# Attention row sums through adding DMAs, maxima subtracted in every step, and roots by a power operation

## The chip, the core and the metric

The kernel runs on one core of a Trainium2 chip. The metric is the device time of one execution in microseconds, as the median of several runs. Engines are named as in the profile: PE is the matrix engine (PEld its weight loads), DVE the vector engine, ACT the scalar engine, POOL the GpSimd engine, SP the engine that issues most DMAs.

## The reference

A decoder layer over x of shape 2 x 2048 x 512 (two batches), in three residual parts. All arithmetic is in f32.

```
h = layernorm(x)                         # mean and variance over 512, eps 1e-5, no weights
Q, K = rope(h Wq^T), rope(h Wk^T)        # 16 heads of 32
V = h Wv^T
x = x + softmax(Q K^T / sqrt(32)) V Wo^T # all 2048 keys, no mask
x = x + gelu_tanh(layernorm(x) ctx^T) ctx    # ctx: 77 x 512 per batch
x = x + clip((layernorm(x) sign(Wf)^T) * scale + bias, -100, 100)
```

## The kernel before

Each batch is worked in two phases. The first, `project_batch`, goes over 16 chunks of 128 rows: normalise, transpose, multiply with the three weights, rotate, and store queries and keys transposed (heads on partitions) in four blocks of 512 columns. The second, `Attention.run`, is the long one.

Attention is cut into 32 units per batch. A unit is a block of 256 queries and a group `g` of four heads. A unit has eight steps; a step treats two chunks of 128 keys for the four heads, in two half-steps (heads 0 and 1, then heads 2 and 3). In a half-step

- `lower` (L501) writes the negated row maxima of the unit into the tile `st` by a small bf16 matmul with ones, where the step asks for it,
- `scores` (L516) accumulates keys times queries on top of it, 128 keys by 256 queries per head and chunk,
- `maxima` (L423) computes scores the other way round (128 queries by 512 keys) for a step ten steps ahead, and DVE reduces them to row maxima (L435),
- ACT takes the exponential of `st` into `pw` (L643), a pool of three buffers,
- POOL adds the two chunks of `pw` into `sm` (L645),
- PE multiplies the weights `pw` of the step before with the values into `acc` (`weigh`, L534).

The row sums of the softmax are the columns of `acc` that `total` (L548) fills: it multiplies `sm` with ones. One half of the 256 columns is done in each half-step, two steps behind. For the last step of a unit the whole 256 columns are done at once. `divide` then copies `acc`, takes reciprocals on DVE (L568) and multiplies on POOL (L571).

To write the maxima only in steps 0 and 4 of a unit, the kernel goes through the keys in an order (`chunk`) in which step 1 takes a chunk of the next key block, and multiplies there with the difference of the two blocks' keys (`key_steps`, L474). Added to the scores already in `st`, that gives the new chunk's scores. The three difference tiles lie in the buffers of the weights wk, wq and wv, so these are loaded again for the second batch.

The maxima of the next unit are split in step 5. DVE reduces them, POOL splits them into three bf16 parts (L444 to L448), and a transposing DMA on SP's queue (L455) turns them into `mrow`, which `lower` reads from the start of the next unit.

The third part, `after_attention`, is everything behind the attention for a block of 512 rows: the output projection, the two norms, the two small networks. It is a generator in a queue; `background` runs one piece of it in each step, and in every other step a further light piece. Its elementwise work lies on POOL as long as attention runs (`side`).

The order on PE, DVE, ACT and POOL in the attention loop is the program order, written by hand (`manual_schedule`).

Roots of the variance are computed without ACT: `rstd_seed` makes a first guess by integer arithmetic on DVE, and `rstd_step` is a Newton step of four operations, taken three times, on POOL (in the last blocks of the program on DVE).

Of the kernel before, what the change touches and what calls it, by code (L numbers as in the profile page):

```python
# [10 lines left out]
BF16 = mybir.dt.bfloat16  # L11
U32 = mybir.dt.uint32
I32 = mybir.dt.int32
AF = mybir.ActivationFunctionType
# [3 lines left out]
P = 128  # L18
# [4 lines left out]
BLK = 512  # L23
# [4 lines left out]
NU = NB * ND * 2  # L28
STEPS = NCH // 2
AHEAD = STEPS + 2  # L30
SCALE = 1.0 / math.sqrt(DK)
# [6 lines left out]
def decoder_layer(  # L38
# [21 lines left out]
    big = ctx.enter_context(tc.tile_pool(name="big", bufs=3))  # L60
    sums = ctx.enter_context(tc.tile_pool(name="sums", bufs=3))
    work = ctx.enter_context(tc.tile_pool(name="work", bufs=5))
# [15 lines left out]


    def load_qkv():  # L80
        return [load_w(w, name) for w, name in ((wk_t, "wk"), (wq_t, "wq"), (wv_t, "wv"))]

    x_next = [load_x(0, 0), load_x(0, 1)]
    qkv = load_qkv()
    cos = const.tile([P, NCH, DK // 2], F32, tag="cos", name="cos")
# [10 lines left out]
    ones = const.tile([P, DK], F32, tag="ones", name="ones")  # L96
    nc.vector.memset(ones, 1.0)


# [32 lines left out]

    def rstd_seed(var, n):
        v = small.tile([P, n], F32, tag=f"v{n}", name="v")
        nc.vector.tensor_scalar(v, var, 1.0, EPS, ALU.mult, ALU.add)
        y = small.tile([P, n], F32, tag=f"rstd{n}", name="rstd")
        t = small.tile([P, n], F32, tag=f"t{n}", name="t")
        nc.vector.tensor_scalar(t.bitcast(I32), v.bitcast(I32), 1, None, ALU.arith_shift_right)
        nc.vector.tensor_scalar(
            y.bitcast(I32), t.bitcast(I32), -1.0, float(0x5F3759DF), ALU.mult, ALU.add  # L140
        )
        return v, y, t

    def rstd_step(engine, v, y, t):
        engine.tensor_mul(t, y, y)
        engine.tensor_mul(t, t, v)
        engine.tensor_scalar(t, t, -0.5, 1.5, ALU.mult, ALU.add)
        engine.tensor_mul(y, y, t)

    def project_batch(b, ahead, att, wk, wq, wv):

        def norm(ch):
            xc = ahead.pop(0)
            if ch + 2 < NCH:
                ahead.append(load_x(b, ch + 2))
            mv = small.tile([P, 2], F32, tag="mv1", name="mv")
            chunk_stats(xc, mv)  # L160
            v, y, t = rstd_seed(mv[:, 1:2], 1)
            for _ in range(3):
                rstd_step(nc.gpsimd, v, y, t)
            off = small.tile([P, 1], F32, tag="off1", name="off1")
            nc.gpsimd.tensor_mul(off, mv[:, 0:1], y)
            nc.gpsimd.tensor_scalar(off, off, -1.0, None, ALU.mult)
            xn = work.tile([P, D], F32, tag="w", name="xn")
            nc.scalar.activation(xn, xc, AF.Identity, bias=off, scale=y)
            return xn
# [93 lines left out]
        att.turn_maxima(0)  # L263
        att.key_steps()

# [18 lines left out]
    def after_attention(b, blk, ot, first, end):  # L284
# [19 lines left out]
        def norm(mv):  # L304
            v, y, t = rstd_seed(mv[:, :, 1], n)
            yield False
            for _ in range(3):
                rstd_step(side(), v, y, t)
                yield False
            off = small.tile([P, n], F32, tag=f"off{n}", name="off")  # L310
            side().tensor_mul(off, mv[:, :, 0], y)
            side().tensor_scalar(off, off, -1.0, None, ALU.mult)
            yield False
            yield False
            for c in range(n):
                xn = work.tile([P, D], F32, tag="w", name="xn2")
                nc.scalar.activation(
                    xn, xs[c], AF.Identity, bias=off[:, c : c + 1], scale=y[:, c : c + 1]
                )
                yield True  # L320
                pt = bank([P, ND, P], "pt2")
                for i in range(ND):
                    nc.tensor.transpose(pt[:, i, :], xn[:, i * P : (i + 1) * P], ident)  # L323
                nc.scalar.copy(ot[:, :, chunks[c]], pt)
                yield c + 1 == n
# [71 lines left out]
    class Attention:  # L397
# [67 lines left out]


        def key_steps(self):
            self.dk = [None] + [
                const.tile([P, ND, BLK], F32, tag=f"w{n}", name=f"dk{n}") for n in "kqv"
            ]  # L470

            def differences(g):
                for kb in range(1, NB):
                    nc.gpsimd.tensor_sub(  # L474
                        self.dk[kb][:, g, :], self.k[kb][:, g, :], self.k[kb - 1][:, g, :]
                    )
                    yield False

            def others():
                for g in range(1, ND):  # L480
                    for _ in differences(g):
                        for _ in range(4):
                            yield False

            for _ in differences(0):
                pass
            queue.append(others())


        @staticmethod  # L490
        def chunk(i, c):
            return (i % NB) * CPB + (i // NB) * 2 + c

        def lower(self, u, heads):
# [13 lines left out]
        def scores(self, u, i, heads, c):  # L510
            qb, g, hf = self.units[u]
            kb, kc = divmod(self.chunk(i, c), CPB)
            keys = self.dk[kb] if kb else self.k[kb]
            for h in heads:
                r = self.rows[h]
                nc.tensor.matmul(  # L516
                    self.st[h][:, c, :],
                    keys[r, g, kc * P : (kc + 1) * P],
                    self.q[qb][r, g, hf * HQ : (hf + 1) * HQ],
                    start=False,  # L520
                    stop=True,
                    skip_group_check=True,
                )


        def weigh(self, step, c):
            u, i, pw, sm = step
            qb, g, hf = self.units[u]
# [3 lines left out]
            for h in range(4):  # L532
                d0 = g * P + h * DK
                nc.tensor.matmul(  # L534
                    acc[self.rows[h], 0, :],
                    self.v[self.chunk(i, c)][:, d0 : d0 + DK],
                    pw[:, h, c, :],
                    start=(i == 0 and c == 0),
                    stop=(i == STEPS - 1 and c == 1),
                    skip_group_check=True,  # L540
                )


        def total(self, step, part):
            u, i, pw, sm = step
            acc = self.acc[u]
            for h in range(4):
                nc.tensor.matmul(  # L548
                    acc[self.rows[h], 1, part],
                    ones,  # L550
                    sm[:, h, part],
                    start=False,
                    stop=(i == STEPS - 1),
                    skip_group_check=True,
# [40 lines left out]
        def run(self):  # L595
            prev = None
            sums_due = None
            ends = []
# [5 lines left out]
            def first_half():  # L604
                if prev is not None:
                    self.weigh(prev, 0)
                if sums_due is not None:
                    self.total(sums_due, slice(0, P))

            def second_half():  # L610
                nonlocal sums_due
                if prev is not None:
                    self.weigh(prev, 1)
                if sums_due is not None:
                    self.total(sums_due, slice(P, HQ))
                sums_due = prev
                if prev is not None and prev[1] == STEPS - 1:
                    self.total(prev, slice(0, HQ))
                    ends.append(self.divide(prev[0]))
                    sums_due = None  # L620

# [10 lines left out]
            for t in range(NU * STEPS):  # L632
                u, i = divmod(t, STEPS)
                pw = big.tile([P, 4, 2, HQ], F32, tag="s", name="pw")
                sm = sums.tile([P, 4, HQ], F32, tag="sm", name="sm")
                for heads, others in (((0, 1), (2, 3)), ((2, 3), (0, 1))):
                    if i % NB == 0:
                        self.lower(u, heads)
                    self.scores(u, i, heads, 0)
# [6 lines left out]
                    if reduce:  # L646
                        reduce()
                    if heads[0] == 0:
                        first_half()
# [5 lines left out]
                    else:  # L655
# [7 lines left out]
                        background(1)  # L663
                prev = (u, i, pw, sm)
            first_half()
# [6 lines left out]
    for b in range(B):  # L672
        att = Attention(b)
        project_batch(b, x_next, att, *qkv)
        if b == 0:
# [3 lines left out]
        if b + 1 < B:  # L679
            x_next = [load_x(b + 1, 0), load_x(b + 1, 1)]  # L680
            qkv = load_qkv()
    alone.append(True)
# [50 lines left out]
```

## Time and profile before

| | us |
|---|---|
| median of 3 runs | 2804.71 (2804.29 to 2805.34) |
| the profiled execution | 2803.13 |
| its span, first to last instruction | 2801.0 |
| granted clock of PE, mean | 0.997 |
| loop of the second batch, by the timeline | 1616 to 2755 |

Busy time of an engine is the union of its instructions' spans. Matmul spans overlap in the pipeline, so the time that a matmul costs is read from the distance of starts, not from its own length. f32 matmuls appear as two records each. A row of the timeline gives start, length, engine, line and operation, the tiles, how many instructions are merged into it, and in brackets how long the engine was idle before it and who ended that.

### The profile page before, as it was taken

The numbers are of one execution on the slowest core, as the hardware profiler recorded it, in microseconds if no ns is written. First come the engines' busy times: TensorE is split into PE (matmuls) and PEld (weight loads), VectorE is DVE, ScalarE is ACT, GpSimd is POOL, SyncE is SP. The second block draws the span as 40 slices with busy tenths as digits, with TensorE's granted clock in tenths as the row PEclk, the third lists the DMA queues.
The fourth block names the chain that finished last, engine by engine and source line by source line (L and its number), as shares of the span: only waits on it lengthen the run. The fifth ranks groups of instructions, "written<-read, shape, count | busy, mean of one in ns | idle before, by whom it ended". The sixth has DMA issues, their size and how long they took to land.

```text
span 2801.0 us, 70846 instructions
## 1 busy us (share of the span) xinstructions
PE 2762.5 (99%) x30748; PEld 1490.8 (53%) x30748; DVE 1714.5 (61%) x3003; ACT 1319.9 (47%) x2391; POOL 1804.3 (64%) x2393
## 2 busy tenths in 40 slices
PE   8999999999999999999999999999999999999997
PEld 4445555555555555555444455555555555555553
DVE  4436777666666766665244467766766666666644
ACT  1114555455546544654322155555555455545542
POOL 4326767567757685767644287766777566857772
PEclk9999999999999999999999999999999999999998
DMA  4000000000100010000201000000000000000000
GB/s 136 20 19 2 5 4 4 4 4 7 30 3 4 4 33 4 4 4 33 72 24 31 15 4 4 4 4 4 4 17 20 4 4 11 26 4 4 18 11 16
DMA packets 41864, 43.56 MB, mean 16 GB/s; under 512 B 24759, under 2 KB 24759, under 8 KB 41553
## 3 DMA queue, kind: packets, MB, share of 16 engines
q1 hardware_dynamic: 41552, 39.05, 4.7%
q8 instruction: 240, 3.93, 0.6%
q14 instruction: 72, 0.58, 0.1%
HBM read 26.58 MB, written 8.39 MB: 12 GB/s over the span
## 4 chain that ended last, share of the span: by engine, by line
PE 96%; DVE 2%; POOL 1%; issue 1%; ACT 0%; DMA 0%; ACTq 0%; DVEq 0%; POOLq 0%
PE st L516 21%; PE acc L534 21%; PE ps L423 18%; PE acc L548 8%; PE pf L363 4%; PE pk L181 4%; PE po L329 4%; PE pv L181 4%; PE pq L181 4%; PE st L501 3%; PE pt L323 1%; PE po L355 1%; PE ph L336 1%; PE ptqk L189 1%; PE pt L174 1%
## 5 line engine op out<-in xcount | busy, mean ns | idle before, releaser
L645 POOL TENSOR_TENSOR sm<-pw 128x512 f32<-128x512 f32 x1024 | 1297.6, 1271 | 628.4 <-ACT pw L643 624.2
L435 DVE TENSOR_REDUCE mx<-ps 128x1 f32<-128x512 f32 x2048 | 1311.8, 682 | 566.6 <-PE ps L423 563.9
L643 ACT ACTIVATE pw<-st 128x512 f32<-128x512 f32 x2048 | 1111.3, 595 | 1004.0 <-PE ps L423 665.9
L423 PE MATMUL ps<-k,q 32*128 32x512 f32 x4096 | 1221.6, 639 | 2.2 <-ACT v L198 1.1
L534 PE MATMUL acc<-pw,v 128*32 128x256 f32 x8192 | 655.6, 391 | 0.0
L548 PE MATMUL acc<-sm,ones 128*32 128x128 f32 x7680 | 392.2, 280 | 1.4 <-POOL sm L645 1.4
L423 PEld LDWEIGHTS ps<-k,q 32*128 32x128 f32 x4096 | 359.4, 183 | 46.7 <-issue 24.3
L534 PEld LDWEIGHTS acc<-pw,v 128*32 128x32 f32 x8192 | 162.4, 108 | 402.3 <-issue 383.2
L548 PEld LDWEIGHTS acc<-sm,ones 128*32 128x32 f32 x7680 | 248.7, 110 | 157.2 <-POOL sm L645 2.7
L516 PE MATMUL st<-q,dkq 32*128 32x256 f32 x2048 | 291.4, 401 | 0.0
L516 PE MATMUL st<-q,dkk 32*128 32x256 f32 x2048 | 291.0, 400 | 0.0
L516 PE MATMUL st<-q,dkv 32*128 32x256 f32 x2048 | 289.9, 400 | 0.0
L516 PE MATMUL st<-q,k 32*128 32x256 f32 x2048 | 265.5, 375 | 0.0
L516 PEld LDWEIGHTS st<-q,dkk 32*128 32x128 f32 x2048 | 175.4, 184 | 90.1 <-issue 48.0
L516 PEld LDWEIGHTS st<-q,dkq 32*128 32x128 f32 x2048 | 172.2, 184 | 79.9 <-issue 55.2
L516 PEld LDWEIGHTS st<-q,dkv 32*128 32x128 f32 x2048 | 174.7, 184 | 68.8 <-issue 37.3
L516 PEld LDWEIGHTS st<-q,k 32*128 32x128 f32 x2048 | 194.4, 187 | 13.6
L214 POOL TENSOR_TENSOR r<-r 128x512 f32<-128x512 f32 x64 | 81.0, 1267 | 184.6 <-DVE r L213 167.0
L568 DVE RECIPROCAL num<-num 128x128 f32<-128x128 f32 x128 | 120.5, 943 | 64.2 <-ACT num L562 64.2
L190 ACT COPY q<-ptqk 128x512 f32<-128x512 f32 x32 | 18.9, 590 | 222.6 <-PE ptqk L189 222.6
L181 PE MATMUL pk<-wk,xnt 128*128 128x512 f32 x256 | 119.7, 611 | 2.7 <-ACT xnt L176 2.7
L363 PE MATMUL pf<-wf,q 128*128 128x512 f32 x256 | 119.1, 609 | 0.0
(99 smaller groups left out, 1963.9 us busy)
## 6 DMA issues: line engine op xcount, KB each, us to landing
x<-in_x_dram SPq DMA_DIRECT2D x64, 256.0 KB, 2.7
out_dram<-x SPq DMA_DIRECT2D x32, 256.0 KB, 2.0
wk<-in_wk_t_dram SPq DMA_DIRECT2D x2, 1024.0 KB, 5.3
wq<-in_wq_t_dram SPq DMA_DIRECT2D x2, 1024.0 KB, 8.0
wv<-in_wv_t_dram SPq DMA_DIRECT2D x2, 1024.0 KB, 12.9
wo<-in_wo_t_dram SPq DMA_DIRECT2D x1, 1024.0 KB, 7.0
wf<-in_wf_t_dram SPq DMA_DIRECT2D x1, 1024.0 KB, 9.1
mrow<-mt SPq DMA_TRANSPOSE x62, 2.3
```

Of the source, the lines that this page charges most:

```text
L181: nc.tensor.matmul(dst, xnt[:, i, :], w[:, i, :], start=(i == 0), stop=(i == ND - 1))
L329: nc.tensor.matmul(ps, ot[:, i, cols], wo[:, i, :], start=(i == 0), stop=(i == ND - 1))
L363: nc.tensor.matmul(pf, ot[:, i, cols], wf[:, i, :], start=(i == 0), stop=(i == ND - 1))
L423: nc.tensor.matmul(ps, self.q[qb][self.rows[h], g, q0 : q0 + P], self.k[kb][self.rows[h], g, :], start=True, stop=True,)
L435: nc.vector.tensor_reduce(mx[:, qc, h, kb : kb + 1], ps, AX.X, ALU.max)
L501: nc.tensor.matmul(self.st[h], ones_b[r, :], mrow[r, None, :].to_broadcast([DK, 2, HQ]), start=True, stop=False, skip_group_check=True,)
L516: nc.tensor.matmul(self.st[h][:, c, :], keys[r, g, kc * P : (kc + 1) * P], self.q[qb][r, g, hf * HQ : (hf + 1) * HQ], start=False, stop=Tr ...
L534: nc.tensor.matmul(acc[self.rows[h], 0, :], self.v[self.chunk(i, c)][:, d0 : d0 + DK], pw[:, h, c, :], start=(i == 0 and c == 0), stop=(i ...
L548: nc.tensor.matmul(acc[self.rows[h], 1, part], ones, sm[:, h, part], start=False, stop=(i == STEPS - 1), skip_group_check=True,)
L568: nc.vector.reciprocal(num[:, 1, part], num[:, 1, part])
L643: nc.scalar.activation(pw[:, h], self.st[h], AF.Exp, scale=SCALE)
L645: nc.gpsimd.tensor_add(sm[:, hs, :], pw[:, hs, 0, :], pw[:, hs, 1, :])
```

## The change

- `total` is no longer called two steps behind. In step 0 POOL's sums go into a tile `first` (one buffer). In steps 1 to 5 they go into `sm` (two buffers), and a DMA issued on POOL's queue adds `sm` into `first` in SBUF. Steps 6 and 7 keep their `sm`. When the unit ends, PE takes the total of `first` in the first half of the next unit's step 0, and those of steps 6 and 7 in the second half, each over all 256 columns.
- `lower` runs in every step. Keys are used as they are, in their own order. `key_steps` is gone, and the weights stay in their buffers for the second batch.
- A root is one addition of eps, one power operation with exponent -0.5 on POOL, and the two operations for the shift. `rstd_seed` and `rstd_step` are gone.

The diff, cut to its core:

```diff
+COLLECTED = STEPS - 2
...
-    sums = ctx.enter_context(tc.tile_pool(name="sums", bufs=3))
+    chain = ctx.enter_context(tc.tile_pool(name="chain", bufs=1))
+    summed = ctx.enter_context(tc.tile_pool(name="summed", bufs=2))
...
+    def scale_and_shift(engine, mv, n):
         y = small.tile([P, n], F32, tag=f"rstd{n}", name="rstd")
+        engine.tensor_scalar(y, mv[:, :, 1], EPS, None, ALU.add)
+        nc.gpsimd.tensor_tensor(y, y, minus_half[:, :n], ALU.pow)
+        off = small.tile([P, n], F32, tag=f"off{n}", name="off")
+        engine.tensor_mul(off, mv[:, :, 0], y)
+        engine.tensor_scalar(off, off, -1.0, None, ALU.mult)
+        return y, off
...
-            kb, kc = divmod(self.chunk(i, c), CPB)
-            keys = self.dk[kb] if kb else self.k[kb]
+            kb, kc = divmod(2 * i + c, CPB)
...
-        def total(self, step, part):
-            u, i, pw, sm = step
+        def total(self, u, sm, last=False):
             acc = self.acc[u]
             for h in range(4):
                 nc.tensor.matmul(
-                    acc[self.rows[h], 1, part],
+                    acc[self.rows[h], 1, :],
                     ones,
-                    sm[:, h, part],
+                    sm[:, h, :],
...
             def first_half():
                 if prev is not None:
                     self.weigh(prev, 0)
-                if sums_due is not None:
-                    self.total(sums_due, slice(0, P))
+                    if prev[1] == STEPS - 1:
+                        self.total(prev[0], due.pop(0))
 
             def second_half():
...
                 if prev is not None:
                     self.weigh(prev, 1)
-                if sums_due is not None:
-                    self.total(sums_due, slice(P, HQ))
...
+                    if prev[1] == STEPS - 1:
+                        while due:
+                            self.total(prev[0], due.pop(0), last=not due)
+                        ends.append(self.divide(prev[0]))
...
-                sm = sums.tile([P, 4, HQ], F32, tag="sm", name="sm")
+                if i == 0:
+                    first = sm = chain.tile([P, 4, HQ], F32, tag="ch", name="first")
+                else:
+                    sm = summed.tile([P, 4, HQ], F32, tag="sm", name="sm")
                 for heads, others in (((0, 1), (2, 3)), ((2, 3), (0, 1))):
-                    if i % NB == 0:
-                        self.lower(u, heads)
+                    self.lower(u, heads)
...
                     nc.gpsimd.tensor_add(sm[:, hs, :], pw[:, hs, 0, :], pw[:, hs, 1, :])
                     if reduce:
                         reduce()
+                    if heads[0] == 2 and 0 < i < COLLECTED:
+                        nc.gpsimd.dma_start(out=first, in_=sm, accum_op=ALU.add)
...
-                prev = (u, i, pw, sm)
+                prev = (u, i, pw)
+                if i == 0 or i >= COLLECTED:
+                    due.append(sm)
```

More of the change, by code (lines that the diff above doesn't have):

```diff
@@ L11 @@
 BF16 = mybir.dt.bfloat16
-U32 = mybir.dt.uint32
-I32 = mybir.dt.int32
 AF = mybir.ActivationFunctionType
@@ L77, in load_w @@
         return t
-    def load_qkv():
-        return [load_w(w, name) for w, name in ((wk_t, "wk"), (wq_t, "wq"), (wv_t, "wv"))]
     x_next = [load_x(0, 0), load_x(0, 1)]
-    qkv = load_qkv()
+    wk = load_w(wk_t, "wk")
+    wq = load_w(wq_t, "wq")
+    wv = load_w(wv_t, "wv")
     cos = const.tile([P, NCH, DK // 2], F32, tag="cos", name="cos")
@@ L97, in decoder_layer @@
     nc.vector.memset(ones, 1.0)
+    minus_half = const.tile([P, CPB], F32, tag="minus_half", name="minus_half")
+    nc.vector.memset(minus_half, -0.5)
     mts = []
@@ L130, in chunk_stats, with project_batch @@
         nc.vector.bn_aggr(mv, st)
-    def rstd_seed(var, n):
-        v = small.tile([P, n], F32, tag=f"v{n}", name="v")
-        nc.vector.tensor_scalar(v, var, 1.0, EPS, ALU.mult, ALU.add)
+    def scale_and_shift(engine, mv, n):
         y = small.tile([P, n], F32, tag=f"rstd{n}", name="rstd")
[L137 to L153, printed above, removed]
+        engine.tensor_scalar(y, mv[:, :, 1], EPS, None, ALU.add)
[4 more added lines that the diff above has]
+        return y, off
+    def project_batch(b, ahead, att):
         def norm(ch):
@@ L158, in norm @@
                 ahead.append(load_x(b, ch + 2))
[L159 to L166, printed above, removed]
+            mv = small.tile([P, 1, 2], F32, tag="mv1", name="mv")
+            chunk_stats(xc, mv[:, 0])
+            y, off = scale_and_shift(nc.gpsimd, mv, 1)
             xn = work.tile([P, D], F32, tag="w", name="xn")
@@ L263, in project_batch @@
         att.turn_maxima(0)
-        att.key_steps()
     alone = []
@@ L304, in norm @@
         def norm(mv):
[L305 to L312, printed above, removed]
+            y, off = scale_and_shift(side(), mv, n)
             yield False
@@ L463, in turn_maxima @@
             self.mrow[u] = mrow.rearrange("p c q -> p (c q)")
[L467 to L492, printed above, removed]
         def lower(self, u, heads):
@@ L517, in scores @@
                     self.st[h][:, c, :],
-                    keys[r, g, kc * P : (kc + 1) * P],
+                    self.k[kb][r, g, kc * P : (kc + 1) * P],
                     self.q[qb][r, g, hf * HQ : (hf + 1) * HQ],
@@ L526, in weigh @@
         def weigh(self, step, c):
-            u, i, pw, sm = step
+            u, i, pw = step
             qb, g, hf = self.units[u]
@@ L535, in weigh @@
                     acc[self.rows[h], 0, :],
-                    self.v[self.chunk(i, c)][:, d0 : d0 + DK],
+                    self.v[2 * i + c][:, d0 : d0 + DK],
                     pw[:, h, c, :],
@@ L541, in weigh @@
                 )
-        def total(self, step, part):
-            u, i, pw, sm = step
+        def total(self, u, sm, last=False):
             acc = self.acc[u]
@@ L548, in total @@
                 nc.tensor.matmul(
-                    acc[self.rows[h], 1, part],
+                    acc[self.rows[h], 1, :],
                     ones,
-                    sm[:, h, part],
+                    sm[:, h, :],
                     start=False,
-                    stop=(i == STEPS - 1),
+                    stop=last,
                     skip_group_check=True,
@@ L596, in run @@
             prev = None
-            sums_due = None
+            due = []
             ends = []
@@ L606, in first_half @@
                     self.weigh(prev, 0)
-                if sums_due is not None:
-                    self.total(sums_due, slice(0, P))
+                    if prev[1] == STEPS - 1:
+                        self.total(prev[0], due.pop(0))
             def second_half():
-                nonlocal sums_due
                 if prev is not None:
                     self.weigh(prev, 1)
-                if sums_due is not None:
-                    self.total(sums_due, slice(P, HQ))
[L616 to L620, printed above, removed]
+                    if prev[1] == STEPS - 1:
+                        while due:
+                            self.total(prev[0], due.pop(0), last=not due)
+                        ends.append(self.divide(prev[0]))
             ordered = tc.manual_schedule(
@@ L673, in decoder_layer @@
         att = Attention(b)
-        project_batch(b, x_next, att, *qkv)
+        project_batch(b, x_next, att)
         if b == 0:
@@ L680, in decoder_layer @@
             x_next = [load_x(b + 1, 0), load_x(b + 1, 1)]
-            qkv = load_qkv()
     alone.append(True)
```

## The prediction

> **What bounds the kernel now.** I read the page first (busy shares, then the chain that ended last), then groups by shape, then the timeline inside the attention loop, last the DMA issues.
>
> ```profile
> span 2801.0 us, 70846 instructions
> PE 2762.5 (99%) x30748; PEld 1490.8 (53%) x30748; DVE 1714.5 (61%) x3003; ACT 1319.9 (47%) x2391; POOL 1804.3 (64%) x2393
> PE 96%; DVE 2%; POOL 1%; issue 1%; ACT 0%; DMA 0%; ACTq 0%; DVEq 0%; POOLq 0%
> ```
>
> TensorE is the bound: 96% of the chain. POOL has a third of the span free. In the attention loop the order on each engine is written by hand, so what matters is how long one half-step (one pair of heads) takes on PE:
>
> ```profile
> 383.31 0.39 PE L501 MATMUL st<-mrow,ones_b 32*128 32x512 bf16 x2
> 384.49 0.64 PE L534 MATMUL acc<-pw,v 128*32 128x256 f32 x8
> 384.94 0.83 PE L548 MATMUL acc<-sm,ones 128*32 128x128 f32 x16
> 385.71 0.48 PE L516 MATMUL st<-q,dkk 32*128 32x256 f32 x2
> 386.78 0.64 PE L534 MATMUL acc<-pw,v 128*32 128x256 f32 x8
> 387.35 0.48 PE L516 MATMUL st<-q,dkk 32*128 32x256 f32 x2
> ...
> 302.04 0.48 PE L516 MATMUL st<-q,dkv 32*128 32x256 f32 x2
> 303.60 0.40 PE L548 MATMUL acc<-sm,ones 128*32 128x128 f32 x8
> 303.94 0.39 PE L501 MATMUL st<-mrow,ones_b 32*128 32x512 bf16 x2
> 305.91 0.39 PE L501 MATMUL st<-mrow,ones_b 32*128 32x512 bf16 x2
> ```
>
> Differences of starts: a half-step without totals and without the maxima matmul (L501) is 387.35-385.71 = 1.64. With a half total it is 303.94-302.04 = 1.90 (its neighbour 1.86, mean 1.88). With both, 305.91-303.94 = 1.97. With L501, a half total and a whole total (16 records) it is 385.71-383.31 = 2.40. So a half total costs 0.24, a whole one 0.43, L501 only 0.09: it runs beside the `ps` matmuls in other rows of the array.
>
> The other thing to read is the route by which the next unit's maxima reach PE:
>
> ```profile
> 312.16 1.28 POOL L645 TENSOR_TENSOR sm<-pw 128x512 f32<-128x512 f32 x1 [0.47 <-ACT pw L643]
> 313.38 0.22 POOL L444 CAST mt<-neg 128x8 bf16<-128x8 f32 x1
> 314.76 1.17 SPq L455 DMA_TRANSPOSE mrow<-mt  x1
> 319.15 0.39 PE L501 MATMUL st<-mrow,ones_b 32*128 32x512 bf16 x2
> 327.80 1.27 POOL L645 TENSOR_TENSOR sm<-pw 128x512 f32<-128x512 f32 x1 [0.47 <-ACT pw L643]
> 344.47 0.22 POOL L444 CAST mt<-neg 128x8 bf16<-128x8 f32 x1
> ```
>
> In step 5 POOL adds, splits the maxima (five small operations, 313.38 to 314.74), SP transposes them, and PE needs them at 319.15. The issue row below says 2.3 us to landing, so they lie there 2.1 us early. Nothing waits today. Casts of consecutive units are 344.47-313.38 = 31.1 apart: a light unit, without work of `after_attention`. The second batch's loop takes 1139 us (1616 to 2755) for 32 units; with 8 light ones the other 24 average 37.1.
>
> ```profile
> x<-in_x_dram SPq DMA_DIRECT2D x64, 256.0 KB, 2.7
> out_dram<-x SPq DMA_DIRECT2D x32, 256.0 KB, 2.0
> wk<-in_wk_t_dram SPq DMA_DIRECT2D x2, 1024.0 KB, 5.3
> mrow<-mt SPq DMA_TRANSPOSE x62, 2.3
> ```
>
> **PE's part of the change, per unit of 16 half-steps.** Removed: 14 half totals, 14 x 0.24 = 3.4, and one whole, 0.43. Added: three whole totals (`first`, steps 6 and 7), 1.3, and L501 in 12 more half-steps, 1.1. PE saves 1.4. The half-steps after `divide` are already longer (DVE's two reciprocals of 0.94 hold back the `ps` tiles); with shorter half-steps they hide less, and I take off 0.2. Net 1.2 x 64 units = 77 us, if PE stays the bound.
>
> **POOL and the DMAs that add.** Each of steps 1 to 5 gets one DMA on POOL's queue: 512 KB of `sm` added into `first`, 320 in all. It starts by waiting for the DMA before it, since both read and write `first`. Behind it in POOL's queue stand the adds of the next step (whose `pw` buffers ACT's exponentials need three steps on), the products of `divide`, the norms of `after_attention` (for which `xn` waits on ACT, with the next exponentials behind it), and in step 5 the split of the maxima. In addition step 7's add needs the buffer that the fifth DMA reads, and PE's total of `first` needs its landing.
>
> Two prices are not in this trace. *d*, POOL's time to issue such a DMA: below by SP's 0.4 for a plain issue of wk (1.64 to 2.07), above by POOL's dearest row of this width (L369, 1.92); I take 1.0, near SP's 1.17 for a transposing issue. *l*, from one issue to the landing that lets the next go: 512 KB lies between 256 KB (2.0 to 2.7) and 1024 KB (5.3). On the line through 2.7 and 5.3 it is 3.6. But the DMA must read both `sm` and `first`, that is 1024 KB, 5.3. I take 4.4, the middle, with 3.0 (out's 2.0 and 1.0 for the issue) and 5.7 as ends. A gain below 3.0 is excluded: the next DMA comes no sooner than the next step's adds, 3.5 us on.
>
> The Trainium skill (DMA: Bandwidth & Descriptors, Anatomy of one DMA) gives some 2.0 us plus bytes over 436 GB/s; by that 256 KB takes an estimated 2.6 (the row says 2.7), 512 KB 3.2 and twice the bytes 4.4, so the sum would be that of the first rival below by the one, and mine by the other. Against this change speaks its section Rules for kernel authors: an accumulating DMA must wait for the earlier one's semaphore, which makes the five serial; no row before shows one.
>
> **A light unit.** From the fifth issue to the next unit's first issue: d 1.0, split 1.36, transposition 2.3 (0.1 for the hand-over); then from L501 to the end of step 1's last add, today 329.07-319.15 = 9.9, to which three whole totals and L501, less the half totals in those steps, add 0.6. That is 15.2. Then four links of l: 4 x 4.4 + 15.2 = 32.8, against 31.1 now and 29.9 for PE alone. So the two steps of slack of the maxima are eaten and PE waits at L501: +1.7, x 16 light units = 27 us.
>
> **A heavy unit.** It has 6.0 us more PE work (37.1-31.1) and 3.4 more on POOL (L367, L369, L370 and the GELU rows, 162 us over 48 units). PE alone: 35.9. The chain: 32.8, a quarter of the 6.0 in steps 0 and 1 (1.5), half of it in steps 2 to 5 less the 0.9 of room that a link has over a step's 3.5 (2.1), and 1.0 for POOL's pieces of up to 3.2 that get between an add and its DMA: 37.4. Some units are held by the chain, some by PE, and the mean of the larger is above either; I take 38.1, +1.0, x 48 = 48 us.
>
> **Roots.** At the start two chunks' roots run on POOL from 5.68 to 9.88; ten of the fourteen operations of each go, one (power) comes. At 0.2 to 1.9 for it, the start saves 1 to 3 us. At the end Newton on DVE (2780.9 to 2784.0, and the norm before it) becomes a hop to POOL and back: 0 to 2 us saved each. In the loop PE hides them. Together -6, between +2 and -8. Key differences: 24 subtractions of 1.27 leave POOL, 18 of them in the loop where POOL waited for ACT: nothing. The second batch's weights are no longer loaded; they landed before 1370.92, where PE waited for `xnt` and not for them: nothing. The new order of key chunks moves no time.
>
> **Sum.** 27 + 48 - 6 = +69 on the profiled execution's 2803.1 (span 2801.0 and 2.1 around it) is 2872; the median of the runs lies 1.6 higher: 2874. PE's 77 us are won and lost again, in waits for the maxima.
>
> **Rivals.** *The DMAs are hidden* (faster): with l of 3.7 or less, 4l + 15.2 is below 29.9 and PE stays the bound. 2804.7-77-6 = 2722 at best; POOL's pieces still cost some, so 2735. For it: 2.0 for 256 KB stored, SBUF on both sides. Against it: two reads, POOL's own issue. Chance 0.23. *The DMAs are slow* (far slower): l of 5.3, as for 1024 KB. Light: 36.4, +5.3 x 16 = 85; heavy: 3.6 more than above less 0.5 of room, +4.1 x 48 = 197; 2804.7 + 282 - 6 = 3080. Chance 0.20. *Issuing binds POOL*: d of 1.9 gives 2.52 + 1.9 = 4.4 per step from POOL's adds alone, no matter when the DMA lands, and 0.9 more in front of the split: 33.7 per light unit, +2.6 x 16, and some 2 x 48 in heavy ones: 2935. Chance 0.10. *My case*, l between 3.7 and 5: 2790 to 2985, chance 0.47.
>
> **How the numbers follow.** Runs before spread over 1 us; 0.2% (5.6 us) can be told from no change. Faster: the first rival and the lower edge of mine, 0.25. Within: 0.05. Slower: 0.70. Range: 2735 to 3080, from the hidden to the slow DMAs; slower cases hold most of it, and their own range is 2811 to 3080.
>
> **What would show it.** PE's share falls below 95%. POOL's adds or the split wait for a DMA; L501 waits, at a unit's start, for `mrow`; casts L444 come some 32.8 apart in light units. The landing of the adding DMA should read 3.4 to 4.4, half-steps without totals about 1.73, totals a quarter of their busy time. Wrong if light units are at 30 or below (hidden), if PE waits but not at unit starts (then `pw` or the total of `first` binds), or if the power operation takes several us and PE waits in the projections.

## The result, and the profile after

The changed kernel takes 3134.07 us (median; 3129.97 to 3142.03) against 2804.5 for the kernel before on the same chip: a ratio of 1.1178, interval 1.1161 to 1.1195. That is 330 us slower where 69 were forecast, and 54 above the upper end of the range. The profiled execution has a span of 3132.1 against 2801.0, 331 more.

The page first: the span, the busy shares, the adding queue (packets, MB, share of 16 DMA engines) and the chain that ended last.

```profile
span 3132.1 us, 61476 instructions
PE 2799.3 (89%) x26140; PEld 1434.9 (46%) x26140; DVE 1676.6 (54%) x2792; ACT 1320.4 (42%) x2391; POOL 2006.3 (64%) x2199
q0 software_dynamic: 46080, 167.79, 27.3%
PE 43%; DMA 32%; POOL 16%; issue 6%; ACT 2%; DVE 1%; POOLq 0%; ACTq 0%; DVEq 0%; SPq 0%
```

PE fell from 99% busy to 89%, and from 96% of the chain to 43%; DMAs, at 0% before, are 32%. PE has 15% fewer matmuls (26140 against 30748) and yet is busy 37 us longer, which already says that some run slowly. The waits (total us, times, longest) name the two places:

```profile
POOL first L594 <- DMA first<-sm: 344.5, 207, 3.8
PE st L450 <- DMA mrow<-mt: 262.9, 46, 11.0
```

POOL waits to issue an adding DMA (L594) until the one before has landed, and PE waits at the maxima matmul (L450) for the transposed maxima. The chain of waits through one light unit of the first batch (start, duration, what) reads as follows:

```profile
310.34 4.43 DMA first<-sm
314.81 0.50 issue
315.31 4.77 DMA first<-sm
...
330.76 0.87 POOL first L594
...
333.02 2.80 DMA mrow<-mt
...
335.87 0.60 PE st L450
...
347.99 4.41 DMA first<-sm
```

The unit is 347.99-310.34 = 37.65 long, and this chain fills it: four links, 330.76-310.34 = 20.42 or 5.1 each, then 17.23 from the fifth issue to the next unit's first. Each link is a landing of about 4.5 **and** some 0.5 between the landing and the next issue. The 17.23 are 2.26 of issue and split, 2.80 of transposition, 0.05 of hand-over and 12.12 from L450 to the next first issue.

What happens in those 12.12 us shows in the windows (length; busy us and instructions of PE, PEld, DVE, ACT, POOL; then the granted clock, the DMA engines' share and GB/s) and the timeline of the same place:

```profile
335.87 0.61 PE L450 MATMUL st<-mrow,ones_b 32*128 32x512 bf16 x2 [6.05 <-DMA mrow<-mt]
329.82:332.18 2.36, 0.00 (x0) 0.00 (x0) 0.61 (x2) 0.59 (x2) 1.30 (x3) 1.00 0.02 7
332.18:335.80 3.62, 0.00 (x0) 0.00 (x0) 0.00 (x0) 0.00 (x0) 3.31 (x6) 0.50 0.85 163
335.80:339.01 3.21, 3.15 (x26) 1.85 (x30) 1.02 (x2) 0.74 (x2) 2.22 (x2) 0.50 0.00 0
335.80:339.50 3.70, 3.63 (x30) 1.95 (x30) 1.29 (x2) 1.09 (x2) 2.22 (x2) 0.57 0.00 0
339.50:343.90 4.40, 4.40 (x66) 2.44 (x63) 1.87 (x3) 2.09 (x4) 2.54 (x2) 1.00 0.00 0
```

PE waited 6.05 us, and in the next 3.7 us it was granted 0.57 of its clock: it is busy 3.63 us for 30 matmuls, where the following 4.4 us hold 66. The 0.57 is a mean: the clock fell to 0.50 at 332.18, 2.4 us after PE's last matmul (329.82), and was back at 1.00 at 339.01, after 3.2 us of work. The Trainium skill (TensorE: Matmul & The Clock Gate, What's actually happening) says that PE's clock is halved after an idle window of about 3.4 us and comes back after as long a stretch of work. The halving agrees; the 2.4 us and the 3.2 us are shorter than that.

Light units average 38.6 us against 31.1 before, heavy ones 41.65 against 37.0 (from one unit's copy of `num` to the next; 14 light and 48 heavy intervals). That is 105 + 224 = 329 us of the 331: the start and the stretch between the batches are 13 longer, the end 11 shorter. In heavy units the same chain is seen on POOL's timeline:

```profile
806.59 0.87 POOL L594 DMA_DIRECT2D first<-sm  x1 [2.13 <-DMA first<-sm]
811.88 0.87 POOL L594 DMA_DIRECT2D first<-sm  x1 [1.90 <-DMA first<-sm]
816.85 0.87 POOL L594 DMA_DIRECT2D first<-sm  x1 [1.59 <-DMA first<-sm]
```

From the second DMA, at 801.04, the links are 5.0 to 5.6 us. The first came at 793.22, further ahead, because pieces of `after_attention` (up to 2.2 us each) stand between a step's adds.

### The profile page after: what moved, and what is told of

It is laid out like the page before. It is cut to its first block, busy times and chain, and to the rows that moved or that the text cites. A ratio compares the mean times of both kernels' runs of the same rounds, so it can differ in the third digit from the quotient of the medians.

```text
span 3132.1 us, 61476 instructions
## 1 busy us (share of the span) xinstructions
PE 2799.3 (89%) x26140; PEld 1434.9 (46%) x26140; DVE 1676.6 (54%) x2792; ACT 1320.4 (42%) x2391; POOL 2006.3 (64%) x2199
## 3 DMA queue, kind: packets, MB, share of 16 engines
q0 software_dynamic: 46080, 167.79, 27.3%
## 4 chain that ended last, share of the span: by engine, by line
PE 43%; DMA 32%; POOL 16%; issue 6%; ACT 2%; DVE 1%; POOLq 0%; ACTq 0%; DVEq 0%; SPq 0%
DMA first<-sm 28%; PE ps L402 8%; POOL sm L590 7%; PE acc L482 6%; PE st L464 5%; PE st L450 4%; DMA mrow<-mt 4%; PE pq L168 4%; PE pk L168 3%; PE pv L168 3%; PE po L308 3%; PE acc L495 3%; POOL first L594 2%; PE pf L342 2%; ACT pw L588 2%
## 5 line engine op out<-in xcount | busy, mean ns | idle before, releaser
L402 PE MATMUL ps<-k,q 32*128 32x512 f32 x4096 | 1327.8, 668 | 1.5 <-DVE mx L414 1.5
L464 PE MATMUL st<-q,k 32*128 32x256 f32 x8192 | 1101.2, 388 | 0.0
L464 PEld LDWEIGHTS st<-q,k 32*128 32x128 f32 x8192 | 816.3, 195 | 47.6
L450 PE MATMUL st<-mrow,ones_b 32*128 32x512 bf16 x2048 | 412.4, 399 | 266.5 <-DMA mrow<-mt 262.9
L594 POOL DMA_DIRECT2D first<-sm x320 | 281.7, 880 | 390.0 <-DMA first<-sm 344.5
L450 PEld LDWEIGHTS <-ones_b 32*128 32x128 bf16 x2048 | 97.2, 91 | 722.0 <-issue 433.4
L590 POOL TENSOR_TENSOR first<-pw 128x512 f32<-128x512 f32 x128 | 161.9, 1268 | 174.6 <-ACT pw L588 95.7
L168 PE MATMUL pq<-wq,xnt 128*128 128x512 f32 x256 | 120.0, 608 | 0.0
L308 PE MATMUL po<-wo,q 128*128 128x512 f32 x256 | 117.9, 604 | 0.0
L168 PE MATMUL pv<-wv,xnt 128*128 128x512 f32 x256 | 115.4, 593 | 0.0
```

The lines of the kernel that those rows point to most:

```text
L168: nc.tensor.matmul(dst, xnt[:, i, :], w[:, i, :], start=(i == 0), stop=(i == ND - 1))
L308: nc.tensor.matmul(ps, ot[:, i, cols], wo[:, i, :], start=(i == 0), stop=(i == ND - 1))
L402: nc.tensor.matmul(ps, self.q[qb][self.rows[h], g, q0 : q0 + P], self.k[kb][self.rows[h], g, :], start=True, stop=True,)
L450: nc.tensor.matmul(self.st[h], ones_b[r, :], mrow[r, None, :].to_broadcast([DK, 2, HQ]), start=True, stop=False, skip_group_check=True,)
L464: nc.tensor.matmul(self.st[h][:, c, :], self.k[kb][r, g, kc * P : (kc + 1) * P], self.q[qb][r, g, hf * HQ : (hf + 1) * HQ], start=False, s ...
L590: nc.gpsimd.tensor_add(sm[:, hs, :], pw[:, hs, 0, :], pw[:, hs, 1, :])
```

## The experiments

All ratios are against the kernel before, run on the same chip. Numbers of lines are those of each kernel. Where units are counted, light means without work of `after_attention`.

### Is it the adding, the bytes, or the number of DMAs?

**A plain copy in place of the add.** Everything else of the changed kernel stays, queue order and waits too.

```
-  nc.gpsimd.dma_start(out=first, in_=sm, accum_op=ALU.add)
+  nc.gpsimd.dma_start(out=first, in_=sm)
```

> The changed kernel with plain copies in place of the adding DMAs (the sums of steps 0 to 4 are lost): same queue, bytes and waits. Theory (reading both operands costs): packets of 4096 bytes fall from 328 ns to about 168, the landing from 4.5 to 3.1 to 3.5, the time to 2850 to 2950. Rival (the landing is POOL's making of descriptors and fixed cost): landing 4.2 or more, 3080 to 3140.

Measured: 2803.7, ratio 0.9996 [0.9986, 1.0007], 46 us below the theory's lower end. The queue's row, the chain by engine and the issue row (KB each, us from issue to landing) of the copying kernel, and after them the issue row of the changed kernel:

```profile
q0 software_dynamic: 46080, 167.79, 14.7%
PE 73%; POOL 14%; DMA 7%; issue 3%; ACT 1%; DVE 1%; POOLq 0%; SPq 0%; ACTq 0%; DVEq 0%
first<-sm POOLq DMA_DIRECT2D x320, 512.0 KB, 2.9
```

```profile
first<-sm POOLq DMA_DIRECT2D x320, 512.0 KB, 4.5
```

The same packets and megabytes take 14.7% of 2803.3 us in the one and 27.3% of 3132.1 in the other: 2.07 times the DMA engines' time. The landing goes from 2.9 to 4.5, and all 330 us of loss hang on that (and on POOL's issue, 0.58 against 0.88 us). That the copying kernel takes the time of the kernel before is a balance: its heavy units are 20 us longer in sum, its start, end and stretch between the batches 17 shorter. The Trainium skill (Collectives: The Full Stack, The bandwidth ceiling: the fold count and why AG ≠ RS ≠ AR) says of the reduce step of collectives that it is half as fast as a copy because it must read two sources; here, in an add from SBUF to SBUF on one core, the factor of 2.07 agrees with it.

**Half the bytes.** The five DMAs carry heads 2 and 3 only.

```
-  nc.gpsimd.dma_start(out=first, in_=sm, accum_op=ALU.add)
+  nc.gpsimd.dma_start(out=first[:, 2:4], in_=sm[:, 2:4], accum_op=ALU.add)
```

> The changed kernel, with each of the five adding DMAs carrying only heads 2 and 3 (256 KB instead of 512; the sums of heads 0 and 1 of steps 1 to 5 are lost); the number of DMAs, their order and everything else as in the changed kernel. Theory (the link is long because the DMA reads both operands and adds, a price by bytes: 4.5 us against 2.9 for the plain copy of the same 512 KB): landing 3.3 or less, the next add's DMA no longer waits, light units 31 to 32, the whole 2800-2860. Rival (a price by DMA: each adding DMA pays some 1.6 us more than a copy, whatever its size): landing 4.0 or more, light units 35.5 or more, 3000-3100.

Measured: 2877.7, ratio 1.0258 [1.0241, 1.0275], 18 us above the theory's upper end and far below the rival; light units average 32.9, where 31 to 32 were forecast. Chain by engine and issue row:

```profile
PE 56%; POOL 28%; DMA 8%; issue 5%; ACT 2%; DVE 1%; POOLq 0%; ACTq 0%; DVEq 0%; SPq 0%
first<-sm POOLq DMA_DIRECT2D x320, 256.0 KB, 3.2
```

The price goes mostly by bytes: 3.2 us land 256 KB, 4.5 land 512, and 256 of the 330 us are gone. The other 73 remain although the serial wait is small (46 us, from 344). Now POOL, not a DMA, is in the chain with PE. An adding DMA costs POOL 0.88 us to issue at either size, 0.3 more than a copy. POOL's busy time is 98 us above that of the copying kernel (2006.5 against 1908.4), which is these 320 x 0.3. The adds of weights have a mean of 1394 ns here and 1271 with plain copies, but that is no second cost: such an add is recorded from 0.6 us after the start of the issue ahead of it, while the issue still runs. PE's waits for the transposed maxima are 86 us, 41 with copies. How the 73 divide between issue and landing was not separated.

**The five DMAs alone.** The kernel before, with the DMAs and the totals of the changed one; the Newton roots and the key differences stay.

```
+  if heads[0] == 2 and 0 < i < COLLECTED:
+      nc.gpsimd.dma_start(out=first, in_=sm, accum_op=ALU.add)
...
   if i % NB == 0:
       self.lower(u, heads)
```

> The kernel before with the five adding DMAs of the changed one; key differences, two maxima matmuls per unit and Newton roots stay. Theory (the DMA chain sets the time, PE's work in the steps is hidden behind it except in steps 0 and 1): 3090 to 3135, near the changed kernel's 3134. Rival (the costs add up, 44 less than the changed kernel by the run with the maxima in each step): 3085 or less.

Measured: 3156.61, ratio 1.1263 [1.1241, 1.1285], 22 above the theory's upper end. Less the 22 us that the roots turn out to be worth (below), it is 3135: the changed kernel's own time. So the maxima matmuls in each step and the missing key differences together do not move it; the DMAs do.

### Is it their being serial?

**Two collecting tiles.** Steps 0 and 1 each start one, the four DMAs go to them in turn, and one more whole total is made. Two pools give up a buffer each for the room.

```
-  if heads[0] == 2 and 0 < i < COLLECTED:
-      nc.gpsimd.dma_start(out=first, in_=sm, accum_op=ALU.add)
+  if heads[0] == 2 and 1 < i < COLLECTED:
+      nc.gpsimd.dma_start(out=firsts[i % 2], in_=sm, accum_op=ALU.add)
```

> The changed kernel with two collecting tiles: steps 0 and 1 fill one each, the DMAs of steps 2 to 5 (four instead of five) go to them in turn, so that a DMA waits for the last but one. To make room the pools work and xpool have one buffer less. Theory (serial waits): hardly any wait of POOL for a landing, light units of 30 to 32, 2800 to 2870 in all. Rival (POOL's time for issuing, 0.88 each, and its adds, 1.40 instead of 1.27, fill POOL): stays above 3000.

Measured: 2905.7, ratio 1.0365 [1.0348, 1.0382], 36 above the forecast. POOL's wait for the DMA before is gone and light units of the second batch are back at 31.2; in the first batch they keep 34 to 36.5. What is left among the waits:

```profile
PE st L450 <- DMA mrow<-mt: 81.9, 37, 7.4
POOL sm L591 <- DMA first<-sm: 44.4, 49, 2.1
```

The adds now wait for a buffer that a DMA still reads (last row). Two tiles give back 228 of the 330 us. Not all of that need be the serial order, since one adding DMA in five is gone too: if each cost a fifth of the 330, that would be 66. Why the two batches differ is open.

**Three DMAs.** Steps 1 to 3 are collected, and steps 4 to 7 keep whole totals, one step behind.

```
-COLLECTED = STEPS - 2
+COLLECTED = STEPS - 4
...
+  if prev[1] >= COLLECTED:
+      self.total(prev[0], due.pop(), last=prev[1] == STEPS - 1)
...
```

> The changed kernel with three adding DMAs (steps 1 to 3); steps 4 to 7 get whole totals on PE in the step after. The third issue comes some 3 us later than the adds allow, and steps 4 and 5 give that back before the split of the maxima. Theory (the length of the serial chain up to the split decides): PE's wait for the maxima in light units goes, light units of 31 to 32, 2790 to 2860. Rival (each DMA costs its share, three fifths of the 330): 2990 to 3020.

Measured: 2915.28, ratio 1.0384 [1.0367, 1.0402], between theory and rival. PE's wait for the maxima has gone, as forecast, since the chain ends two steps sooner. What it pays in its place is PE's own work, five whole totals per unit instead of three, and a new wait of PE, 59.6 us, at a total for the add before it.

### What lies between the fifth DMA and the next unit

**Split ahead of the fifth DMA.**

```
+  if heads[0] == 2 and (t + AHEAD) % STEPS == STEPS - 1 and u + 1 < NU:
+      self.split_maxima(u + 1)
+      self.turn_maxima(u + 1)
   if heads[0] == 2 and 0 < i < COLLECTED:
       nc.gpsimd.dma_start(out=first, in_=sm, accum_op=ALU.add)
```

> The changed kernel; in step 5 the split of the next unit's maxima stands ahead of the fifth adding DMA on POOL instead of behind it. Theory (the five DMAs wait for one another, and PE's first matmul of a unit waits for the maxima behind them): the split no longer waits for the fourth landing, a light unit falls from 37.6 to some 35, PE's wait at the maxima matmul from 263 us to under 150, the time to 2970 to 3050. Rival (the DMAs slow POOL's adds and PE by contention, the order in the queue does not matter): 3115 to 3150.

Measured: 3059.19, ratio 1.0902 [1.0886, 1.0919]: 75 us better than the changed kernel, 9 above the forecast. The mechanism did less than the time says. Light units were to fall to 35; they average 37.4 against 38.6, and in the first batch 37.7 against 38.0. PE's wait at the maxima was to be under 150 us; it is 198. Of the 75, some 52 come from the heavy units. The chain of one light unit, its windows after the wait (columns as above) and the transposition's issue row, here and then in the changed kernel, show why not more:

```profile
327.23 4.25 DMA mrow<-mt
331.52 0.61 PE st L450 x2
344.94 4.40 DMA first<-sm
331.00:334.00 3.00, 2.48 (x18) 1.62 (x22) 0.35 (x1) 0.07 (x1) 1.96 (x2) 0.50 0.12 22
334.00:338.00 4.00, 4.00 (x38) 2.08 (x34) 1.29 (x3) 1.25 (x3) 1.79 (x2) 0.58 0.00 0
mrow<-mt SPq DMA_TRANSPOSE x62, 4.5
```

```profile
mrow<-mt SPq DMA_TRANSPOSE x62, 2.7
```

The transposition now takes 4.25 us instead of 2.80: it is issued at the same moment as the fifth adding DMA, where in the changed kernel it came 2.3 us behind it. PE still waits, and is granted 0.50 to 0.58 in the 7 us afterwards, so that L450 to the next first issue takes 13.42 instead of 12.12.

**The same, with the maxima turned by PE.** At the end of step 7 PE transposes them, as the kernel already does for the first unit; SP's DMA goes.

```
-  if u > 0:          # SP's transposing DMA
+  if False:          # PE, as for unit 0
...
   if i == STEPS - 1 and u + 1 < NU:
+      self.turn_maxima(u + 1)
```

> The kernel with the split ahead of the fifth adding DMA (3059), with the maxima turned by PE at the end of step 7 instead of by SP's transposing DMA. Theory (the moved split brought only half of what was forecast because the transposition then ran beside the fifth adding DMA, 4.25 instead of 2.80 us, and PE still waited and lost clock): 2950-3010, the PE wait for the maxima gone, light units about 34.5 to 36, set by five serial links and the total. Rival (the five links and what follows them set the unit wherever the transposition is done): 3040-3070.

Measured: 2987.7, ratio 1.0659 [1.0635, 1.0682], inside the theory. The chain and the wait that takes over:

```profile
306.69 4.43 DMA first<-sm
341.82 4.43 DMA first<-sm
PEld acc L495 <- DMA first<-sm: 107.6, 40, 4.3
```

The unit shown is 35.13 (light units average 36.3, a little above the forecast), and what PE waits for is now the total of `first` after the fifth landing: five serial links and that total set the unit. Beyond this the collected sum itself is late.

**Work for PE in the wait.** Six pairs of matmuls, overwritten later, ahead of a light unit's first L450.

```
+  for _ in range(idle):          # 6 in a light unit's first half-step
+      for h in heads:
+          nc.tensor.matmul(self.st[h], self.k[0][r, g, :P], self.k[1][r, g, :], ...)
```

> The changed kernel, with six pairs of extra 32-row matmuls put on PE ahead of the first maxima matmul of a light unit (their results are overwritten, so the computation is the same). Theory (after the 6 us wait for the maxima PE is granted about half its clock, 0.57 in the window after it, and that costs about 1.5 us in each light unit): the granted clock of the first half-steps after the wait stays near 1.0, the light units go from 37.5 to about 36 and the whole from 3134 to 3100-3118. Rival (those half-steps are long because they wait for DVE and ACT to fill up again, or the chain of DMAs alone sets the unit's length): 3130-3145, with the clock up and the units as long as before.

Measured: 3113.93, ratio 1.1104 [1.1089, 1.1120]: 20 us less than without, by doing more. Its window after the wait (columns as above) and the chain:

```profile
335.70:339.50 3.80, 3.77 (x52) 2.32 (x55) 1.70 (x3) 1.39 (x3) 3.49 (x3) 1.00 0.02 4
335.73 0.39 PE st L460 x2
346.38 4.52 DMA first<-sm
```

52 matmuls where there were 30, at a granted 1.00, and 10.65 us from the maxima matmul to the next first issue instead of 12.12. So the slow clock costs about 1.5 us in this unit. The total does not show that price in every unit: the 14 light units, which alone have the extra matmuls, give only 7 of the 20 us. In the first batch they average 37.1 instead of 38.0, the shortest 36.0 and 35.8; in the second they stay at 39, with landings of up to 6.65 us. The heavy units, without extra matmuls, are 16 us shorter in sum in the first batch and 8 longer in the second, and the stretch between the batches is 4.5 shorter. What moves those was not tried.

### PE's own part

**The maxima matmul in every step, without the differences**, in the kernel before:

```
-  if i % NB == 0:
-      self.lower(u, heads)
+  self.lower(u, heads)
```

> The kernel before with the maxima matmul in every step, keys in their own order, no key differences, no second load of the weights; totals on PE as before. By the half-steps of before (0.09 us each, 12 more per unit, 64 units) +70: 2865 to 2890. Rival (the matmul hides wholly in the other rows of the array): 2800 to 2810.

Measured: 2849.07, ratio 1.0162 [1.0147, 1.0177], +44: between forecast and rival, 0.06 us for each of the 768 matmuls added instead of 0.09.

**One whole total per step instead of two halves**, in the kernel before:

```
-  self.total(sums_due, slice(0, P))
...
-  self.total(sums_due, slice(P, HQ))
+  self.total(sums_due, slice(0, HQ))
```

> The kernel before, with each total done once per step over 256 columns instead of twice over 128, still two steps behind. By the half-steps of before a half total costs 0.24 and a whole one 0.43: 7 x 0.05 x 64 = 22 saved, 2775 to 2790. Rival (the longer half-step makes the maxima tiles or ACT late): 2800 or more.

Measured: 2863.83, ratio 1.0208 [1.0192, 1.0223], +58 where a gain of 22 was forecast: wrong in sign. Starts of the first score matmul in successive half-steps of that kernel:

```profile
308.88 0.48 PE L516 MATMUL st<-q,dkk 32*128 32x256 f32 x2
310.52 0.48 PE L516 MATMUL st<-q,dkk 32*128 32x256 f32 x2
312.85 0.48 PE L516 MATMUL st<-q,dkq 32*128 32x256 f32 x2
```

Without a total 1.64, with a whole one 2.33: a whole total costs 0.69 here, where one half-step of before gave 0.43. The price is not the same in every place: in the copying kernel it is 0.42 (shown in the next section). What makes the difference was not shown.

### The roots

**Power roots alone**, in the kernel before:

```
-  v, y, t = rstd_seed(mv[:, :, 1], n)
-  yield False
-  for _ in range(3):
-      rstd_step(side(), v, y, t)
-      yield False
...
+  y, off = scale_and_shift(side(), mv, n)
```

> The kernel before with the roots of the changed one, nothing else. Prediction's step: -6, 2796 to 2801. Rival (the hop to POOL and the power operation, 0.57 in the changed kernel, cost as much as they save): 2803 to 2808.

Measured: 2782.95, ratio 0.992 [0.9905, 0.9935]: 22 us faster, and the best version here. The profiled executions differ by 17 us and place these: 11.4 us between the last copy of `num` and the end, 3.1 before the first, 2.8 in the loops and between them. The power operation is 565 ns for 128x1 and 1040 for 128x4.

**Newton in one piece**, in the kernel before, to see whether the smaller number of pieces in the background queue is what pays:

```
   v, y, t = rstd_seed(mv[:, :, 1], n)
-  yield False
   for _ in range(3):
       rstd_step(side(), v, y, t)
-      yield False
```

> The kernel before, its Newton roots kept, with the root's steps issued as one piece of the background queue (four pieces fewer per norm); the arithmetic is the same. Theory (the power root's gain of 22 us over the kernel before comes mostly from fewer pieces in the queue, so that less background work is left after the loop): 2785-2797. Rival (it comes from the shorter root itself): 2801-2808.

Measured: 2825.64, ratio 1.0078 [1.0064, 1.0091], 21 slower; neither forecast. The end after the last copy of `num` does get 4.4 us shorter (45.0 against 49.4), but the two loops grow by 15.6 and 6.9 and the stretch between them by 6.6. Fewer pieces alone are not the gain: with the Newton root kept, they lengthen the loops.

## Why the prediction was wrong

**What held.** The mechanism was the forecast one: DMAs in series, a chain through split and transposition to L450, PE's saving lost in waits for the maxima at a unit's start. PE's share fell below 95%, the split waits for a DMA, half-steps with L450 and no total take 1.75 and 1.79 (forecast 1.73), by the starts of L450 in the changed kernel:

```profile
304.49 0.39 PE L450 MATMUL st<-mrow,ones_b 32*128 32x512 bf16 x2
306.24 0.39 PE L450 MATMUL st<-mrow,ones_b 32*128 32x512 bf16 x2
308.03 0.39 PE L450 MATMUL st<-mrow,ones_b 32*128 32x512 bf16 x2
```

The landing, at 4.4 the boldest estimate, measured 4.5; it was the middle between two readings, 3.6 and 5.3, with no row of an adding DMA, so that it came so close is luck. d, at 1.0, fits too: 0.88, and issue and split together took 2.26 for the forecast 2.36.

**The step that failed first: "four links of l: 4 x 4.4".** The text defined l as running to the landing "that lets the next go", as if the next went then. The chain shows another 0.5 us of issue before each. A link is 5.1, so the four are 2.8 longer: 2.1 by the four hand-overs, 0.7 by landings of 4.57 on average.

**The second: K, "that is 15.2".** It measured 17.23. The transposition took 2.80 for 2.3 and 0.1 of hand-over (its median is 2.3 before and with plain copies, so the adding DMA beside it lengthens it), and the largest part, L450 to the next first issue, 12.12 for "9.9 ... add 0.6". With PE kept busy it was 10.65, so 10.5 was right for a PE at full clock; in the unit shown 1.5 is the clock that PE lost in the very wait that the prediction foresaw. A wait of several us was priced at its length alone.

Both corrections give 32.8 + 2.8 + 2.0 = 37.6 for a light unit; the unit shown has 37.65.

**The third follows from them: heavy units "38.1, +1.0".** With the forecast's own formula and the measured terms, 37.65 + 1.5 + (3.0 less the room of a link over a step, now 1.6) + 1.0 = 41.55; measured 41.65. That it fits to 0.1 is partly luck, since light units average 38.6 and not 37.65. The prediction had the chain and PE about equal in heavy units (37.4 against 35.9) and so a small excess. Some 4 us more on the chain came through almost whole, 48 times: this is 224 of the 329 us, and why an error of 5 us in a sum of 33 became one of 260 in the total.

**PE's 77 us.** PE's own account was nearly right, as the copying kernel shows in units where PE waits for nothing. Its copies of `num` in two such units, and PE's L450 in three half-steps in a row:

```profile
354.55 0.58 ACT L509 COPY num<-acc 128x512 f32<-128x512 f32 x1 [0.38 <-PE acc L495]
384.62 0.59 ACT L509 COPY num<-acc 128x512 f32<-128x512 f32 x1 [0.38 <-PE acc L495]
414.69 0.58 ACT L509 COPY num<-acc 128x512 f32<-128x512 f32 x1 [0.38 <-PE acc L495]
379.68 0.39 PE L450 MATMUL st<-mrow,ones_b 32*128 32x512 bf16 x2
381.87 0.39 PE L450 MATMUL st<-mrow,ones_b 32*128 32x512 bf16 x2
384.48 0.39 PE L450 MATMUL st<-mrow,ones_b 32*128 32x512 bf16 x2
```

The units take 30.07 where 29.9 were forecast and 31.1 were needed before. A half-step with one whole total takes 2.19 and one with two 2.61, against 1.77 with none: 0.42 for a whole total, as forecast. What failed is the first rival's time. A landing of 2.9 meets its condition (3.7 or less), so it should have taken 2735; it took 2804. PE's busy time falls by 47 us (2715.9 against 2762.5), but its idle time rises by 49 (87.4 against 38.5), 41 of it at L450 for the transposed maxima. Light units average 31.1, between 30.1 and 33.8, and heavy ones 37.4, which is 0.4 more than before. So even plain copies hold PE up at the start of some units, where the prediction let a landing below 3.7 cost nothing. What delays the maxima there was not separated.

**Roots: -6 against -22.** The forecast looked at the start and the end and let PE hide the rest. The start was right (3.1 for "1 to 3"); the stretch after the loop gave 11.4 where "0 to 2 us saved each" was written, and the loops and the stretch between them gave 2.8. (On POOL twelve of a root's fourteen operations went and two came, not ten and one.) The direction was right, the term a quarter of its size. Why the end gains so much is only partly shown: fewer pieces gave 4.4 of it.

**The range.** The slow-DMA rival, 3080, had the right shape for the wrong reason (a landing of 5.3). As an end it carried neither the hand-over nor the clock, and so stopped 54 short. The hand-over belongs to every link and the clock to every long wait of PE, and neither had a bound in the text.

## What to carry to other kernels

Price a chain of dependent DMAs as its landings plus the time from each landing to the next issue, and compare that with the period of the loop before trusting any saving on the bounding engine: what the chain exceeds the period by is lost in every pass, and here it cost most where chain and engine had looked balanced. When a forecast says that TensorE will wait several us in each pass, look at the granted clock behind the wait and add the slow stretch to the price. To find out what a collecting DMA costs, swap the add for a copy; the cost of its parts cannot be read off the changed kernel alone.

## Not expected of the hardware

- An adding DMA from SBUF to SBUF takes 2.07 times the DMA engines' time of a copy of the same packets, lands 512 KB in 4.5 us against 2.9, and takes POOL 0.88 us to issue against 0.58.
- After a wait of 6.05 us PE's granted clock was 0.50 for its first 3.2 us of work. With extra matmuls in the wait it was 1.00, and the stretch behind the wait was 1.5 us shorter in the unit shown.
- A transposing DMA took 2.3 us before the change, 2.7 when issued 2.3 us behind an adding DMA, and 4.5 when issued together with one (medians).
- A whole total cost 0.69 us in one kernel's half-step and 0.42 in another's; two halves in two half-steps cost 0.24 each before the change. Swapping halves for wholes in the kernel before cost 58 us; why the price differs is open.
